# A two-layer graph-attention kernel: transposes of the layers' inputs by VectorE and through DRAM

## The chip, the cores and the metric

The kernel runs on one core of one Trainium2 chip. A core has TensorE (PE, matrix products, with weight loads listed as PEld), VectorE (DVE), ScalarE (ACT), GpSimd (POOL) and SyncE (SP), which here only issues DMAs; each engine works through its own queue in order. The metric is device microseconds of one execution, and lower is better.

## The reference

128 graphs with 128 nodes of 512 features each, all float32, and one adjacency mask per graph. Layer 0 is masked attention with 4 heads of 64, layer 1 is a layer norm with gamma and beta followed by masked attention with 8 heads of 64; in layer 1 each node also sees itself. Each layer adds its input and is normalised.

```python
# layer 0
q, k, v = heads(x @ Wq), heads(x @ Wk), heads(x @ Wv)            # 4 heads of 64
sim  = where(adj, q @ k.T * 64**-0.5, -float32_max)
x    = layernorm(x + (softmax(sim) @ v) @ Wo + bo)
# layer 1
h = (x - mean(x)) * rsqrt(var(x) + 1e-5) * gamma + beta
q, k, v = heads(split(h @ w_qkv.T))                              # 8 heads of 64
sim  = where(adj | eye, q @ k.T * 64**-0.5, -1e9)
out  = layernorm(x + (softmax(sim) @ v) @ w_out.T + b_out)
```

## The kernel before

Work goes in groups of two graphs (`G = 2`, 64 groups). `step(s)` is run for s = 0 to 66 and is a software pipeline written out by hand: the order of the calls in it is the order of the instructions on every engine. In step s layer 0's q, k and v of group s are made (`chunk(0, s, n)`, n = 0 to 3), layer 0's attention runs for group s-1, layer 1's inputs are turned and projected for group s-2 (`transposed(1, s-2)`, `product`), and layer 1's attention runs for group s-3. A step has two halves, one for each graph of the pair; `scores(k)` opens each, with k = 2s and 2s+1.

Within a half, `scores` (L303) makes the score matrices on PE, copies them under the mask on DVE, takes the row maxima, and queues the exponentials for ACT in a list `later`, which `flush` empties: layer 0's exponentials leave inside `scores`, layer 1's at the next `flush()`. `attend(k-1)` (L371) multiplies the previous half's probabilities with v and has ACT copy the result to aT; `normalised(k)` divides by the sums on POOL; `residual(l, k-1)` (L400) multiplies aT with the output weights, adds the input and makes the statistics; `norms` (L435) writes layer 0's result h, or stores layer 1's result y.

PE needs operands with the contracted axis on the partitions, so three things are turned. The probabilities are turned in `blocks` (L351): DVE turns 32 by 32 blocks within their partitions, and sixteen DMAs from SBUF to SBUF put the blocks in their places. The inputs of both layers are turned in `transposed` (L164) by PE against an identity matrix into PSUM, and ACT copies the result to xT, for layer 1 with gamma and beta applied on the way. Layer 1's weights are loaded and turned by PE in `load_transposed` (L101), one block of 128 rows for each call of `p` in the first steps; each block's DMA is issued when its turn comes.

Layer 1's projections are seven products per pair (`product`, L200; a Strassen scheme, in which graph 0 and graph 1 and two halves of the features and weights form 2 by 2 blocks). Each adds into one of three PSUM tiles, named a, c and f in `INTO`. ACT copies tile a out after products 1, 6, 7 and 4, and the later ones add to it. The sums of inputs that they need (`xs`) are made on POOL at the end of `transposed`.

All DMAs are issued by SP, in program order, so one that has to wait holds up all behind it.

Of the kernel before, what the change touches and what calls it, by code (L numbers as in the profile page):

```python
# [10 lines left out]
F32 = mybir.dt.float32  # L11
# [6 lines left out]
P = 128  # L18
# [9 lines left out]
def kernel(ctx: ExitStack, tc: tile.TileContext, x, adj, wq, wk, wv, wo, bo,  # L28
# [11 lines left out]
    two = ctx.enter_context(tc.tile_pool(name="two", bufs=2))  # L40
    three = ctx.enter_context(tc.tile_pool(name="three", bufs=3))
    four = ctx.enter_context(tc.tile_pool(name="four", bufs=4))
    ps_mm = ctx.enter_context(tc.tile_pool(name="ps_mm", bufs=6, space=PSUM))
    ps_st = ctx.enter_context(tc.tile_pool(name="ps_st", bufs=1, space=PSUM))

# [3 lines left out]
    def mm_tile(name):  # L49
        return ps_mm.tile([P, 512], F32, tag="mm", name=name)  # L50
# [4 lines left out]
    def flush(n=0):  # L55
        while len(later) > n:
            later.pop(0)()
# [42 lines left out]

    def load_transposed(dst, src, name, scaled=0):  # L101
        rows, cols = src.shape

        def part(r):
            raw = three.tile([P, cols], F32, tag="h", bufs=10, name=f"{name}_{r}")
            nc.sync.dma_start(raw, src[r * P:(r + 1) * P, :])
            pt = mm_tile(f"{name}t_{r}")
            for c in range(cols // P):
                nc.tensor.transpose(pt[:, c * P:(c + 1) * P], raw[:, c * P:(c + 1) * P], ident)
            to = dst[:, :, r * P:(r + 1) * P]  # L110
            pt = pt.rearrange("p (c f) -> p c f", f=P)
            if r * P < scaled:
                nc.scalar.activation(to, pt, AF.Copy, scale=SCALE)
            elif r % 2:
                nc.scalar.copy(to, pt)
            else:
                nc.vector.tensor_copy(to, pt)

        setup.extend(lambda r=r: part(r) for r in range(rows // P))

    def load_gamma_beta():
        nc.sync.dma_start(gb_raw[:KC], gamma.rearrange("(c p) -> c p", p=P))
        nc.sync.dma_start(gb_raw[KC:], beta.rearrange("(c p) -> c p", p=P))
        pt = mm_tile("gb_t")
        nc.tensor.transpose(pt[:, :2 * KC], gb_raw, ident[:2 * KC, :2 * KC])
        nc.vector.tensor_copy(gb, pt[:, :2 * KC])
# [25 lines left out]
                nc.vector.tensor_sub(t4, b21, t2)  # L152

    load_transposed(w1, w_qkv, "w_qkv", scaled=INNER[1])
    setup.append(load_gamma_beta)
    load_transposed(wo1, w_out, "w_out")
    setup.append(weight_sums)

# [2 lines left out]
    RATIO, H, XT, QK, V = {}, {}, {}, {}, {}  # L161


    def transposed(l, g):  # L164
        if not 0 <= g < NG:
            return
        xT = one.tile([P, KC, T], F32, tag=f"xT{l}", name=f"xT{l}_{g}")
        for c0 in range(0, KC, 2):
            pt = mm_tile(f"xt{l}_{g}_{c0}")
            for c in range(c0, c0 + 2):  # L170
                for b in range(G):
                    src = X[g][:, b] if l == 0 else H[g, b]
                    o = ((c - c0) * G + b) * N
                    nc.tensor.transpose(pt[:, o:o + N], src[:, c * P:(c + 1) * P], ident)  # L174
            if l == 0:
                nc.scalar.copy(xT[:, c0:c0 + 2, :], pt.rearrange("p (c t) -> p c t", t=T))  # L176
            else:
                for c in range(c0, c0 + 2):
                    nc.scalar.activation(xT[:, c, :], pt[:, (c - c0) * T:(c - c0 + 1) * T],  # L179
                                         AF.Identity, bias=gb[:, KC + c:KC + c + 1],  # L180
                                         scale=gb[:, c:c + 1])
        XT[l, g] = xT
        if l == 1:
            xs = one.tile([P, 4, KH, N], F32, tag="xs", name=f"xs_{g}")
            a = xT.rearrange("p (h c) (b n) -> p b h c n", h=2, b=2)
            s1, s2, s3, s4 = (xs[:, i] for i in range(4))
            for o, a0, a1, op in ((s1, a[:, 1, 0], a[:, 1, 1], ALU.add),
                                  (s2, s1, a[:, 0, 0], ALU.subtract),
                                  (s3, a[:, 0, 0], a[:, 1, 0], ALU.subtract),
                                  (s4, a[:, 0, 1], s2, ALU.subtract)):  # L190
                nc.gpsimd.tensor_tensor(o, a0, a1, op=op)
            XS[g] = xs


    XS, ACC, EV = {}, {}, {}
# [69 lines left out]
    def chunk(l, g, n):  # L265

        if not 0 <= g < NG:
            return
        xT = XT[l, g]
        I = INNER[l]  # L270
        nq = I // P
        if n == 0:
            QK[l, g] = two.tile([P, 2 * nq, T], F32, tag=f"qk{l}", name=f"qk{l}_{g}")
            V[l, g] = two.tile([P, G, I], F32, tag=f"v{l}", name=f"v{l}_{g}")
        pm = mm_tile(f"p{l}_{g}_{n}")
        if n < nq:
            for f in (2 * n, 2 * n + 1):
                for c in range(KC):
                    nc.tensor.matmul(pm[:, (f % 2) * T:(f % 2 + 1) * T],  # L279
                                     W[l][:, c, f * P:(f + 1) * P], xT[:, c, :],  # L280
                                     start=(c == 0), stop=(c == KC - 1))
            dst = QK[l, g][:, 2 * n:2 * n + 2, :]
            src = pm.rearrange("p (f t) -> p f t", t=T)
        else:
            b = n - nq
            for c in range(KC):
                nc.tensor.matmul(pm[:, :I], xT[:, c, b * N:(b + 1) * N], W[l][:, c, 2 * I:3 * I],  # L287
                                 start=(c == 0), stop=(c == KC - 1))
            dst, src = V[l, g][:, b, :], pm[:, :I]
        if (n + l) % 2:  # L290
            nc.scalar.copy(dst, src)
        else:
            nc.vector.tensor_copy(dst, src)
# [57 lines left out]
    def blocks(k):  # L351


        both = members(k)
        if not both:
            return
        slots = {0: (0, HEADS[0]), 1: (HEADS[0], HEADS[0] + HEADS[1])}
        t = one.tile([P, 4, sum(HEADS), 32], F32, tag="turned", name=f"turned_{k}")
        pT = one.tile([P, 4, sum(HEADS), 32], F32, tag="pT", name=f"pT_{k}")
        for l, g, b in both:  # L360
            lo, hi = slots[l]
            sm = SM.pop((l, g, b)).rearrange("p s k (q r) -> p q (s k) r", r=32)
            nc.vector.transpose(t[:, :, lo:hi, :], sm)  # L363
            PT[l, g, b] = pT[:, :, lo:hi, :]
        lo, hi = slots[both[0][0]][0], slots[both[-1][0]][1]
        for q in range(4):
            for a in range(4):
                nc.sync.dma_start(pT[32 * q:32 * q + 32, a, lo:hi, :],  # L368
                                  t[32 * a:32 * a + 32, q, lo:hi, :])

    def attend(k):  # L371
        both = members(k)
# [16 lines left out]
    def addend(l, k):  # L389

        for _, g, b in [m for m in members(k) if m[0] == l]:
            if l == 0:
                xin = X[g][:, b, :]
            else:
                xin = H.pop((g, b))
                nc.scalar.activation(xin, xin, AF.Copy, scale=RATIO.pop((g, b)))
            nc.gpsimd.tensor_tensor(xin, xin, (bias0, bias1)[l], op=ALU.add)
            XB[l, g, b] = xin

    def residual(l, k):  # L400
        for _, g, b in [m for m in members(k) if m[0] == l]:
# [4 lines left out]
                nc.tensor.matmul(pm, aT[:, c * P:(c + 1) * P], WO[l][:, c, :],  # L406
                                 start=(c == 0), stop=(c == nk - 1))
            if l == 0:
                y = three.tile([P, E], F32, tag="h", bufs=10, name=f"h_{g}_{b}")
            else:  # L410
                y = two.tile([P, E], F32, tag="y", name=f"y_{g}_{b}")
            nc.vector.tensor_add(y, pm, XB.pop((l, g, b)))  # L412
# [31 lines left out]
    def step(s):  # L444
        def c(n):
            chunk(0, s, n)

        def p(kind, *which, g=s - 2):
            for i in which:
                product(kind, g, i)  # L450
            if setup:
                setup.pop(0)()

        k = 2 * s
        scores(k)
        addend(0, k - 1)
        c(0)
        flush()
        p("", g=-1)
        attend(k - 1)  # L460
        normalised(k)
        addend(1, k - 1)
        c(1)
        p("", g=-1)
        residual(0, k - 1)
        blocks(k)
        p("v", 4, 3, g=s - 3)
        flush()
        residual(1, k - 1)
        transposed(1, s - 2)  # L470
        flush()
        c(2)
        p("qk", 1, 2)
        load(s + 2)
        k += 1
        scores(k)
        addend(0, k - 1)
        p("qk", 6, 5)
        flush()
        attend(k - 1)  # L480
        normalised(k)
        addend(1, k - 1)
        p("qk", 7)
        c(3)
        residual(0, k - 1)
        blocks(k)
        p("qk", 4)
        flush()
        residual(1, k - 1)
        p("qk", 3)  # L490
        flush()
        p("v", 1, 2)
        transposed(0, s + 1)
        p("v", 6, 5, 7)

    transposed(0, 0)
    for s in range(NG + 3):
        step(s)
    assert not setup
# [34 lines left out]
```

## Time and profile before

| | |
|---|---|
| median of 3 runs | 3177.49 us (3176.98 to 3177.89) |
| the profiled execution | 3175.61 us, its span 3173.8 us |
| mean granted TensorE clock | 0.989 |
| busy: PE, DVE, POOL, ACT | 97%, 54%, 43%, 41% of the span |
| matmul instructions | 20801 |
| DMA queue of SP | 159088 packets, 176.84 MB, 19.6% of 16 engines' span |
| transposes of inputs on PE (L174) | 1024, 68.1 us for layer 0 and 67.1 us for layer 1 |

The span runs from the first to the last instruction of that execution. A float32 product takes two matmul instructions (L406 is called 768 times and shows 1536); a transpose takes one. Matmuls are pipelined, so their busy times overlap at the edges; the distance from one start to the next is what one costs in the queue. In the timeline and in the chain of waits, a line gives the start, the length, the engine, the line of the kernel and how many instructions are merged. In the list of DMAs, the last number is the median time from issue to landing.

### The profile page before, as it was taken

To read this page: it belongs to the slowest core of one execution; us is meant where nothing else is said; L and a number is where in the kernel's file an instruction comes from. 1 tells how busy PE (TensorE), PEld (TensorE's weight loads), DVE (VectorE), ACT (ScalarE), POOL (GpSimd) and SP (SyncE) were. 2 spreads that over 40 slices of the span, in tenths; PEclk is the share of its full clock that TensorE was granted. 3 is DMA by queue.
4 is the path that set the end of the run, shared out by engine and by line. 5 is a ranking of instruction groups with operands and counts; after the bars stand their busy time and mean duration, and the time that the engine had idled before them with its cause. 6 is when DMAs were issued, how large, how long until landed. Compare 5 with 4: busy or idle time off the path is not lost.

```text
span 3173.8 us, 57024 instructions
## 1 busy us (share of the span) xinstructions
PE 3092.1 (97%) x20801; PEld 2488.4 (78%) x20801; DVE 1703.0 (54%) x2968; ACT 1285.6 (41%) x4492; POOL 1349.5 (43%) x1799
## 2 busy tenths in 40 slices
PE   5999999999999999999999999999999999999986
PEld 4788878878878878878878878878878888888864
DVE  3355555555555555555555555555555555555553
ACT  2344444444444434434434434444444443443432
POOL 1344444444444444444444444444444444444442
PEclk8999999999999999999999999999999999999998
DMA  3112112112112212212212212212212212212111
GB/s 121 32 54 62 55 53 63 55 52 64 55 51 62 58 50 63 58 49 62 60 48 63 61 48 62 61 48 61 62 48 60 61 50 59 57 54 59 49 42 44
DMA packets 159367, 180.49 MB, mean 57 GB/s; under 512 B 54632, under 2 KB 123760, under 8 KB 159088
## 3 DMA queue, kind: packets, MB, share of 16 engines
q1 hardware_dynamic: 159088, 176.84, 19.6%
q8 instruction: 166, 2.72, 0.4%
q14 instruction: 113, 0.93, 0.1%
HBM read 42.47 MB, written 33.55 MB: 24 GB/s over the span
## 4 chain that ended last, share of the span: by engine, by line
PE 95%; DVE 1%; SPq 1%; ACT 1%; POOL 0%; DMA 0%; issue 0%; POOLq 0%; DVEq 0%; ACTq 0%
PE o L406 21%; PE qka L229 15%; PE p L279 14%; PE qkf L229 7%; PE p L287 7%; PE va L229 7%; PE sc L314 6%; PE av L383 6%; PE qkc L229 3%; PE xt L174 3%; PE vf L229 3%; PE vc L229 2%; SPq L368 1%; ACT sm L339 1%; DVE sm L327 0%
## 5 line engine op out<-in xcount | busy, mean ns | idle before, releaser
L348 POOL TENSOR_TENSOR sm<-sm,rec 128x512 f32<-128x512 f32 (+1 forms) x256 | 376.1, 1469 | 1058.8 <-DVE rec L347 1058.8
L339 ACT ACTIVATE sm<-sm,nmax 128x128 f32<-128x128 f32 x1536 | 595.2, 389 | 488.7 <-DVE nmax L330 434.2
L406 PE MATMUL o<-wo,aT 128*128 128x512 f32 x1536 | 709.7, 598 | 9.2 <-ACT aT L387 9.2
L406 PEld LDWEIGHTS o<-wo,aT 128*128 128x128 f32 x1536 | 289.0, 192 | 270.0 <-issue 248.8
L279 PE MATMUL p<-xT,w 128*128 128x256 f32 x2048 | 478.7, 387 | 1.1 <-ACT xT L176 1.1
L279 PEld LDWEIGHTS p<-xT,w 128*128 128x128 f32 x2048 | 380.5, 191 | 67.0 <-issue 10.8
L419 POOL TENSOR_SCALAR ve<-mv 128x1 f32<-128x1 f32 x256 | 56.0, 219 | 698.5 <-DVE mv L416 698.5
L339 ACT ACTIVATION_READ_ACCUMULATOR sm<-sm,nmax 128x1 f32 x1536 | 286.7, 187 | 0.0
L327 DVE COPY_PREDICATED sm<-m,sc 128x512 f32<-128x512 uint8 (+1 forms) x512 | 270.6, 581 | 25.3 <-PE sc L314 7.4
L229 PEld LDWEIGHTS qkf<-xs,w 128*128 128x128 f32 x2048 | 243.8, 192 | 30.1 <-issue 30.1
L229 PE MATMUL qka<-xs,wsqk 128*128 128x128 f32 x2048 | 262.6, 281 | 0.0
L255 ACT COPY ev<-va 128x256 f32<-128x256 f32 x192 | 71.5, 372 | 460.8 <-PE va L229 443.9
L363 DVE STREAM_TRANSPOSE turned<-sm 128x512 f32<-128x512 f32 (+1 forms) x256 | 235.7, 957 | 35.4 <-issue 27.4
L229 PEld LDWEIGHTS qka<-xs,wsqk 128*128 128x128 f32 x2048 | 238.2, 191 | 18.7 <-issue 10.8
L347 DVE RECIPROCAL rec<-total 128x4 f32<-128x4 f32 (+1 forms) x256 | 47.5, 185 | 378.8 <-ACT sm L339 378.8
L412 DVE TENSOR_TENSOR h<-o,x 128x512 f32<-128x512 f32 x128 | 88.5, 692 | 300.1 <-PE o L406 298.2
L229 PE MATMUL qkf<-xs,w 128*128 128x128 f32 x2048 | 249.4, 275 | 0.0
L330 DVE TENSOR_REDUCE nmax<-sm 128x4 f32<-128x512 f32 (+1 forms) x256 | 244.0, 953 | 8.8
L287 PE MATMUL p<-w,xT 128*128 128x256 f32 x1024 | 246.5, 384 | 0.0
L179 ACT ACTIVATE xT<-xt,gb 128x256 f32<-128x256 f32 x256 | 123.7, 563 | 280.2 <-PE xt L174 280.2
L383 PE MATMUL av<-pT,v 128*64 128x128 f32 x3072 | 198.9, 278 | 24.7 <-DMA pT<-turned 22.4
L383 PEld LDWEIGHTS av<-pT,v 128*64 128x64 f32 x3072 | 167.0, 138 | 55.2 <-issue 40.8
(84 smaller groups left out, 4713.4 us busy)
## 6 DMA issues: line engine op xcount, KB each, us to landing
pT<-turned SPq DMA_DIRECT2D x1984, 48.0 KB, 1.9
x<-in_x_dram SPq DMA_DIRECT2D x64, 512.0 KB, 3.8
out_dram<-y SPq DMA_DIRECT2D x128, 256.0 KB, 2.2
w_qkv<-in_L_gnn_w_qkv_dram SPq DMA_DIRECT2D x12, 256.0 KB, 5.6
m<-in_adj_dram SPq DMA_DIRECT2D x64, 32.0 KB, 3.5
pT<-turned SPq DMA_DIRECT2D x64, 32.0 KB, 1.8
pT<-turned SPq DMA_DIRECT2D x64, 16.0 KB, 1.8
w_out<-in_L_gnn_w_out_dram SPq DMA_DIRECT2D x4, 256.0 KB, 3.2
```

The lines of the kernel that those rows point to most:

```text
L179: nc.scalar.activation(xT[:, c, :], pt[:, (c - c0) * T:(c - c0 + 1) * T], AF.Identity, bias=gb[:, KC + c:KC + c + 1], scale=gb[:, c:c + 1])
L229: nc.tensor.matmul(o, lhsT, rhs, start=first and n == 0, stop=n == len(todo) - 1, skip_group_check=True)
L279: nc.tensor.matmul(pm[:, (f % 2) * T:(f % 2 + 1) * T], W[l][:, c, f * P:(f + 1) * P], xT[:, c, :], start=(c == 0), stop=(c == KC - 1))
L287: nc.tensor.matmul(pm[:, :I], xT[:, c, b * N:(b + 1) * N], W[l][:, c, 2 * I:3 * I], start=(c == 0), stop=(c == KC - 1))
L314: nc.tensor.matmul(ps[h % 2][:, h // 2, :], qk[r, h // 2, t], qk[r, H_ // 2 + h // 2, t], start=True, stop=True)
L327: nc.vector.copy_predicated(sm[:, s], mask[:, None, :].to_broadcast([P, K, N]), ps[s][:, :K, :])
L330: nc.vector.tensor_reduce(nmax, sm, AX.X, ALU.max, negate=True)
L339: nc.scalar.activation(sm[:, s, k, :], sm[:, s, k, :], AF.Exp, bias=nmax[:, s, k:k + 1], accum_out=total[:, s, k:k + 1])
L348: nc.gpsimd.tensor_tensor(sm, sm, rec[:, :, :, None].to_broadcast([P, 2, K, N]), op=ALU.mult)
L363: nc.vector.transpose(t[:, :, lo:hi, :], sm)
L383: nc.tensor.matmul(o.rearrange("p (a r) -> p a r", r=32), v[:, b, h * D:(h + 1) * D], pT[:, :, s * K + kk, :], start=True, stop=True)
L406: nc.tensor.matmul(pm, aT[:, c * P:(c + 1) * P], WO[l][:, c, :], start=(c == 0), stop=(c == nk - 1))
```

## The change

Neither layer's input is turned on PE any more, except group 0 of layer 0 (`first_transposed`). `turn(l, g, b)` has DVE turn 32 by 32 blocks of one graph; after the second graph, `put` stores the whole turned tile (512 KB) to a scratch tile in DRAM with one DMA, and `arrive(l, g)` fetches it into place with four DMAs of 32 partitions each (`fetch`). Layer 0's result is used as it arrives: xT0 has the layout [node, graph, feature block], so that PE reads a column at every eighth float. Layer 1's arrives in a tile `raw`; `finish(g)` applies gamma and beta on ACT, writes xT1 and makes xs on POOL. The probabilities take the same way: one put and four fetches (`probs_arrive`) in place of the sixteen DMAs.

The order in `step` changes with it. All seven v products of a group now run in the first half of the next step, the seven qk products in the second half. Layer 0's `turn` stands after `addend(1, k-1)` of the first half, its `arrive` before `residual(0, k-1)`. Layer 1's graph 0 is turned in the second half of a step, its graph 1 in the first half of the next; `arrive(1, s-2)` follows `probs_arrive` of the first half, and `finish(s-2)` stands between `scores` and `c(2)` of the second. The loads of gamma, beta and all blocks of layer 1's weights are issued before the first step, into buffers that the steps use later.

```diff
 def load_transposed(dst, src, name, scaled=0):
+    raws = []
+    for r in range(rows // P):
+        if name == "w_qkv" and r < 8:
+            raw = three.tile([P, cols], F32, tag="h", bufs=8, name=f"{name}_{r}")
+        else:
+            if r % 4 == 0:
+                four_rows = two.tile([P, 4, cols], F32, tag="qk1", name=f"{name}_{r}")
+            raw = four_rows[:, r % 4]
+        nc.sync.dma_start(raw, src[r * P:(r + 1) * P, :])
+        raws.append(raw)
     def part(r):
-        raw = three.tile([P, cols], F32, tag="h", bufs=10, name=f"{name}_{r}")
-        nc.sync.dma_start(raw, src[r * P:(r + 1) * P, :])
+        raw = raws[r]
...
-def transposed(l, g):            # PE transposes into PSUM, ACT copies to xT (L164-L192)
...
+def put(t, name):
+    scr = dram.tile(list(t.shape), F32, tag=name.split("_")[0], name=name)
+    nc.sync.dma_start(scr, t)
+    return scr
+def fetch(dst, scr):
+    src = scr.rearrange("(a r) q x -> r q a x", r=32)
+    for q in range(4):
+        nc.sync.dma_start(dst[32 * q:32 * q + 32], src[:, q])
+def turn(l, g, b):
+    if b == 0:
+        TURNED[l] = one.tile([P, 4, G * KC * 32], F32, tag=f"turned{l}", name=f"turned{l}_{g}")
+    src = (X[g][:, b] if l == 0 else H[g, b]).rearrange("p (c a i) -> p a c i", a=4, i=32)
+    if l == 0:
+        dst = TURNED[l].rearrange("p a (i b c) -> p a b c i", b=G, c=KC)[:, :, b]
+    else:
+        dst = TURNED[l].rearrange("p a (b c i) -> p a b c i", b=G, c=KC)[:, :, b]
+    nc.vector.transpose(dst, src)
+    if b == G - 1:
+        SCR[l] = put(TURNED[l], f"scr{l}_{g}")
+def arrive(l, g):
+    if l == 0:
+        xT = XT[0, g] = two.tile([P, N, G, KC], F32, tag="xT0", name=f"xT0_{g}")
+        fetch(xT.rearrange("p (a j) b c -> p a (j b c)", a=4), SCR[0])
+    else:
+        RAW[g] = one.tile([P, 4, G, KC, 32], F32, tag="raw", name=f"raw_{g}")
+        fetch(RAW[g].rearrange("p a b c i -> p a (b c i)"), SCR[1])
+def finish(g):
+    raw = RAW[g]
+    xT = XT[1, g] = one.tile([P, KC, T], F32, tag="xT1", name=f"xT1_{g}")
+    for c in range(KC):
+        nc.scalar.activation(xT[:, c, :].rearrange("p (b a j) -> p b a j", b=G, a=4),
+                             raw[:, :, :, c, :].rearrange("p a b j -> p b a j"),
+                             AF.Identity, bias=gb[:, KC + c:KC + c + 1], scale=gb[:, c:c + 1])
...
 def chunk(l, g, n):
-    nc.tensor.matmul(pm[:, (f % 2) * T:(f % 2 + 1) * T],
-                     W[l][:, c, f * P:(f + 1) * P], xT[:, c, :], ...)
+    nc.tensor.matmul(o.rearrange("p (b n) -> p b n", b=G),
+                     W[l][:, c, f * P:(f + 1) * P],
+                     xT[:, :, :, c].rearrange("p n b -> p b n"), ...)
-    nc.tensor.matmul(pm[:, :I], xT[:, c, b * N:(b + 1) * N], W[l][:, c, 2 * I:3 * I], ...)
+    nc.tensor.matmul(pm[:, :I], xT[:, :, b, c], W[l][:, c, 2 * I:3 * I], ...)
...
 def blocks(k):
-    for q in range(4):
-        for a in range(4):
-            nc.sync.dma_start(pT[32 * q:32 * q + 32, a, lo:hi, :], t[32 * a:32 * a + 32, q, lo:hi, :])
+    t, pT = (u[:, :, lo:hi, :].rearrange("p a h i -> p a (h i)") for u in (t, pT))
+    SCR["p"] = pT, put(t, f"scrp{hi - lo}_{k}")
+def probs_arrive(k):
+    if members(k):
+        fetch(*SCR["p"])
...
 def step(s):
     normalised(k)
     addend(1, k - 1)
+    turn(0, s + 1, 0)
+    turn(0, s + 1, 1)
     c(1)
     p("", g=-1)
+    arrive(0, s + 1)
     residual(0, k - 1)
     blocks(k)
-    p("v", 4, 3, g=s - 3)
+    p("v", 1, 2, g=s - 3)
     flush()
+    turn(1, s - 2, 1)
+    probs_arrive(k)
+    arrive(1, s - 2)
+    p("v", 6, 5, g=s - 3)
     residual(1, k - 1)
-    transposed(1, s - 2)
+    p("v", 7, g=s - 3)
     flush()
-    c(2)
-    p("qk", 1, 2)
+    p("v", 4, 3, g=s - 3)
     load(s + 2)
     k += 1
     scores(k)
     addend(0, k - 1)
-    p("qk", 6, 5)
+    finish(s - 2)
+    c(2)
     flush()
     attend(k - 1)
     normalised(k)
     addend(1, k - 1)
-    p("qk", 7)
-    c(3)
+    p("qk", 1)
     residual(0, k - 1)
     blocks(k)
+    p("qk", 2)
+    flush()
+    turn(1, s - 1, 0)
+    probs_arrive(k)
+    p("qk", 6, 5, 7)
+    residual(1, k - 1)
     p("qk", 4)
     flush()
-    residual(1, k - 1)
     p("qk", 3)
-    flush()
-    p("v", 1, 2)
-    transposed(0, s + 1)
-    p("v", 6, 5, 7)
+    c(3)
```

## The prediction

> **What bounds the kernel now.** I read the page first: which engine is busy, and at which clock.
>
> ```profile
> PE 3092.1 (97%) x20801; PEld 2488.4 (78%) x20801; DVE 1703.0 (54%) x2968; ACT 1285.6 (41%) x4492; POOL 1349.5 (43%) x1799
> ...
> PEclk8999999999999999999999999999999999999998
> ```
>
> TensorE (PE) has work 97% of the span at full clock, so a microsecond off its queue counts only while nothing makes it wait. Next I read the chain of work that ended last, in one step in the middle.
>
> ```profile
> 1505.56 1.54 PE sc L314 x24
> 1507.10 3.65 PE p L279 x16
> 1510.74 1.46 PE av L383 x24
> 1512.21 3.65 PE p L279 x16
> 1515.86 1.72 PE o L406 x4
> ...
> 1522.73 0.87 PE xt L174 x8
> ...
> 1528.91 1.54 PE sc L314 x24
> ...
> 1549.91 0.87 PE xt L174 x8
> ```
>
> Every piece is PE. The next step's scores start 47.8 us after 1505.5 (1553.30 in PE's timeline). The xt lines, the transposes of both layers' inputs, are 2 x 0.87 = 1.74 us of it. The third view is the timeline of the second half-step, for what stands behind PE.
>
> ```profile
> 1519.54 1.84 DVE L363 STREAM_TRANSPOSE turned<-sm 128x512 f32<-128x512 f32 x2 [0.22 <-issue]
> ...
> 1521.45 10.93 SPq L368 DMA_DIRECT2D pT<-turned  x16
> ...
> 1523.21 1.93 ACT L179 ACTIVATE xT<-xt,gb 128x256 f32<-128x256 f32 x4 [4.36 <-PE xt L174]
> ...
> 1528.84 1.61 PE L314 MATMUL sc<-qk 64*128 64x128 f32 x24
> ...
> 1531.26 0.40 ACT L339 ACTIVATE sm<-sm,nmax 128x128 f32<-128x128 f32 x1 [3.46 <-DVE nmax L330]
> ...
> 1534.20 0.40 ACT L339 ACTIVATE sm<-sm,nmax 128x128 f32<-128x128 f32 x1 [0.82 <-DVE rec L347]
> ...
> 1537.29 0.83 ACT L387 COPY aT<-av 128x256 f32<-128x256 f32 x2
> ...
> 1539.29 1.02 PE L406 MATMUL o<-wo,aT 128*128 128x512 f32 x2
> ```
>
> The reader should see ScalarE's (ACT's) order: layer 0's exponentials begin 2.42 us after the scores, layer 1's at 5.36, aT is copied at 8.45, and PE needs it only at 10.45. That slack of 1.6 us (the layer-0 copy takes 0.35) exists because qk products 6, 5 and 7 and a chunk stand between the scores and o. The sixteen pT DMAs take 10.93 us to issue and just make the next attend.
>
> **The change part by part.** I count t from a step's first scores, u from its second.
>
> *Transposes off PE.* 127 of 128 groups go: -1.74 us a step. ACT loses layer 0's copies (L176, 68.8 us in all); they lay beside PE and gain nothing. VectorE (DVE) gains four transposes a step of 0.71 us (the 128x512 row of L363). Layer 0's two fall into 3.36 us in which DVE waits for o (t=8.8 to 12.2), so cost nothing; layer 1's follow the h norm.
>
> *Product order, first half.* All seven v products now follow o of layer 0 (0.865 each). Product 4 stands directly behind 7 and adds to the same PSUM tile that ACT must copy first. Product 7's matmuls end 1.03 us after they start, ACT starts 0.09 later (1505.56 to 1505.65 in that timeline) and takes 0.37, so with a hand-over product 4 starts at 1.55 instead of 0.865: +0.7. The first half is 1.54+3.65+1.46+3.65+1.72+7x0.865+3.43 = 21.5, so u=0 is t=22.2.
>
> *Product order, second half.* Between scores and o stand only c(2), attend and product 1: 1.54+1.73+1.46+1.78 = 6.5 us. ACT's order is layer 0's exponentials, the four of `finish`, layer 1's exponentials, aT. This is the wait that replaces the transposes. At the earliest: 3.98 (layer 0 done) + 1.93 (L179 x4) + 3.09 (layer 1, 1534.20 to 1537.29) + 0.35 + 0.1 hand-over = 9.45. Floor of the stall: 2.9 us a step.
>
> *The trip through DRAM.* `finish` also needs layer 1's raw tile, behind everything on SP's queue. Its prices have these rows:
>
> ```profile
> x<-in_x_dram SPq DMA_DIRECT2D x64, 512.0 KB, 3.8
> out_dram<-y SPq DMA_DIRECT2D x128, 256.0 KB, 2.2
> ...
> w_out<-in_L_gnn_w_out_dram SPq DMA_DIRECT2D x4, 256.0 KB, 3.2
> ```
>
> A put of 512 KB is the 256 KB store's 2.2 plus 256 KB at 347 GB/s (319 GB/s at a share of 0.92 in the first 20 us) = 2.95; of 768 KB, 3.7. An issue is 0.63 (sixteen in 10.1 to 10.9). Layer 0's turned tile is ready at t=10.25, put by 13.2, its four fetches issued by 15.75. The probabilities' put starts when blocks ends (t=15.9) and lands at 19.6; layer 1's put is queued at 17.6 (after the h norm and 0.71). Eight fetches follow, probabilities first: the last starts at 19.6+7x0.63 = 24.0. A 256 KB load lands in 3.2, a 48 KB pT copy in 1.9; I take 3.2, the one that reads DRAM. Probabilities land at 24.7, before attend at u=3.27 (t=25.5): hidden, by 0.8. Layer 1 lands at 27.2, u=5.0. Then o is at 5.0+1.93+3.09+0.35+0.1 = 10.5 and the stall **4.0 us** a step.
> The ends: 2.9 where raw lands before u=3.98. At the other, DVE's strided writes doubled (+1.4), puts of 3.8 and 4.5 (the 512 KB load's price), landings of 3.8 and issues of 0.68: layer 1 lands near t=31.3, u=9.1, stall 8.1. The odd half's probabilities have some 5 us to spare and are hidden.
>
> *The clock.* The 4.0 us are two gaps: before product 1 (1.3, for `finish`'s first two pieces) and before o (about 2.6). PE's timeline shows what gaps do:
>
> ```profile
> 134.53 0.98 PE L174 MATMUL xt<-ident,h 128*128 128x128 f32 x7 [2.78 <-DVE h L437]
> 135.35 3.27 PE L287 MATMUL p<-w,xT 128*128 128x256 f32 x8
> ...
> 3129.53 3.70 PE L406 MATMUL o<-wo,aT 128*128 128x512 f32 x8 [2.32 <-ACT aT L387]
> ```
>
> After 2.78 us idle the granted clock fell to 0.50 for some 3 us and eight matmuls took 3.27 instead of 1.89; after 2.32 us it did not fall. A gap between the two pays about 1.5 us in half of the steps: +0.75; ends 0 and 1.65. [...]
>
> *Strided columns.* Layer 0's xT0 has a column every 8 floats; no operand of before is read so. Ends: nothing, or the 32 matmuls of c(0) and c(1) doubled, +7.3 us a step, plus about 1.3 in c(3) for strided weight loads; 64 steps give +550. I take nothing, since the nearest row, pT read in runs of 32 (av: 198.9 us for 3072 matmuls; the contiguous sc: 207.5 for 3072), shows no surcharge for a split pattern; that row is far. [...]
>
> *Weights in one go.* In the first 75 us PE waited 11.2 us for gamma/beta and 15.7 us for w_out, both queued on SP behind pT issues. They now come before any put. A first put, fetch and attend trip with no work over it takes some back: -20 us; ends 0 and -35.
>
> *Sum.* 61 steps hold both layers and c(2): 61 x (-1.74 + 0.7 + 4.0 + 0.75) = +226. With -20: 3175.6 (the profiled execution) + 206 = 3381.6. The median of the runs shown is 1.9 above that execution, so 3384.
>
> **The rivals.**
> *Faster: the wait before o does not appear.* Then 127 x 0.87 = 110 and 20 at the start come off, and 64 x 0.7 = 45 for product 4 stay: 3177.5-110-20+45, about 3092. It decides where ACT delivers aT within 7.5 us of the second scores, 1.04 after PE asks: the point at which wait plus 0.7 equals 1.74. Against it: even before, with no `finish` in ACT's queue, aT of layer 0 was not copied before 8.45+0.35 = 8.8. For it: nothing in these rows, only the chance that a piece of PE's queue is longer than summed.
> *Little slower: only the floor.* Raw is there by u=3.98 and the clock stays up: 61 x (-1.74+0.7+2.9) = +113, start -35: about 3255. Both puts would have to land in little more than the 256 KB store's 2.2.
> *Strided columns cost.* 3384 + 550 = 3935 for a full doubling, about 3620 for half. For: eight floats between columns is the new thing in PE's reading. Against: pT's split runs.
> *DRAM trips much later.* Stall 8.1 and the clock loss in every step: 61 x 8.7 = +531, about 3709.
>
> **How the numbers follow.** Forecast as summed 0.62, its own range 3255 to 3710; strided columns 0.22 (3600 to 3935); between no change and 3255, 0.08; faster 0.07; within 0.2% (about what a measurement of this kernel can tell from no change) 0.01. So slower has 0.92. From 3240 to 3830 leaves out faster, most of the little-slower case and the top of the strided one: just under 2 in 10.
>
> **What would show it.** Right: the waits list ACT aT under PE's o near the scores' second half, some 2 to 3 us in about 61 places, and PE's product 1 on ACT's xT; ACT's `finish` waits for the DMA of raw; a v product waits 0.7 for ACT; PE's share falls to about 90% with DVE near 1880 us busy; the step is some 51.5 us. Strided cost: c(0) takes over 3.7 us for its 16. Wrong: if aT is early, or raw lands before u=4. If attend waits for pT, the put is dearer than 3.7.

## The result and the profile after

The changed kernel takes 3889.23 us (median of 4 runs, 3877.59 to 3894.92) against 3177.55 before: 1.2235 times as long, 95% interval 1.2206 to 1.2264, or 712 us more. The forecast, 3384 in 3240 to 3830, had the direction and missed the size; the time lies above the range, 46 us under the 3935 of the rival that strided columns cost. The profiled execution took 3891.53 us, its span 3889.7.

First the page's busy times and its row of the granted clock.

```profile
PE 3610.7 (93%) x19785; PEld 2500.5 (64%) x19785; DVE 1923.8 (49%) x3223; ACT 1239.9 (32%) x4365; POOL 1349.3 (35%) x1799
...
PEclk9999999999999999999999999999999999999998
```

PE runs 1016 matmul instructions fewer (the transposes) and is busy 519 us longer, at a clock that is nine tenths or more in all of these coarse slices but the last. So most of the loss is no wait: single instructions have become longer. The groups, with shapes kept apart, say which (sum, mean ns of one, idle time before them and what ended it); first three of them before, then after:

```profile
L279 PE MATMUL p<-xT,w 128*128 128x256 f32 x2048 | 478.7, 387 | 1.1 <-ACT xT L176 1.1
...
L287 PE MATMUL p<-w,xT 128*128 128x256 f32 x1024 | 246.5, 384 | 0.0
...
L287 PEld LDWEIGHTS p<-w,xT 128*128 128x128 f32 x1024 | 187.6, 193 | 20.9
```

```profile
L330 PE MATMUL p<-xT,w 128*128 128x256 f32 x2048 | 976.0, 645 | 3.0 <-ACT xT L221 3.0
L460 PE MATMUL o<-wo,aT 128*128 128x512 f32 x1536 | 745.9, 623 | 169.3 <-ACT aT L441 169.3
...
L339 PE MATMUL p<-w,xT 128*128 128x256 f32 x1024 | 286.7, 423 | 0.0
...
L339 PEld LDWEIGHTS p<-w,xT 128*128 128x128 f32 x1024 | 255.5, 335 | 8.9 <-issue 1.0
```

L330 (L279 before) makes layer 0's q and k and streams xT0 as its moving operand: 478.7 us and 387 ns before, 976.0 and 645 now. L339 (L287) has xT0 as the loaded weights: a load takes 335 ns instead of 193, and its 1024 matmuls are 40 us busier. Together that is 538 us of the 712. Most of the rest is in the waits (engine, tile and line, releaser, us in all, times, longest); before, o waited 9.2 us for aT in all:

```profile
PE o L460 <- ACT aT L441: 169.3, 67, 5.8
...
ACT xT L231 <- DMA raw<-scr: 59.0, 57, 13.3
...
PE va L279 <- ACT ev L305: 37.5, 65, 4.4
...
PE qka L279 <- ACT xT L231: 33.5, 39, 2.8
...
PE av L437 <- DMA pT<-scrp: 19.7, 8, 6.0
```

These are the waits that the prediction named, in its places: about one a step before o for aT, of 2.5 us on average, `finish` for raw, a v product for ACT, and in 39 steps product 1 for `finish`; the probabilities' trip is on time but for 8 places. PE's timeline shows both kinds of loss in one step.

```profile
2022.56 1.61 PE L366 MATMUL sc<-qk 64*128 64x128 f32 x24
2024.10 7.62 PE L330 MATMUL p<-xT,w 128*128 128x256 f32 x16
2031.65 1.53 PE L437 MATMUL av<-pT,v 128*64 128x128 f32 x24
2033.11 7.62 PE L330 MATMUL p<-xT,w 128*128 128x256 f32 x16
2040.56 1.90 PE L460 MATMUL o<-wo,aT 128*128 128x512 f32 x4
...
2049.18 1.03 PE L279 MATMUL va<-wsv,xs 128*128 128x256 f32 x4
2050.72 1.13 PE L279 MATMUL va<-wsv,xT 128*128 128x256 f32 x4 [0.52 <-ACT ev L305]
...
2052.64 1.61 PE L366 MATMUL sc<-qk 64*128 64x128 f32 x24
2054.18 2.29 PE L339 MATMUL p<-w,xT 128*128 128x256 f32 x8
2056.40 1.53 PE L437 MATMUL av<-pT,v 128*64 128x128 f32 x24
2057.90 2.32 PE L279 MATMUL qka<-xT,w 128*128 128x128 f32 x16
2062.70 3.45 PE L460 MATMUL o<-wo,aT 128*128 128x512 f32 x4 [2.48 <-ACT aT L441]
2065.99 1.95 PE L279 MATMUL qkc<-xT,w 128*128 128x128 f32 x16
...
2082.26 1.61 PE L366 MATMUL sc<-qk 64*128 64x128 f32 x24
```

The step is 59.7 us long (2022.56 to 2082.26) where it was 47.8. Start to start, c(0) takes 7.55 and c(1) 7.45 instead of 3.65 and 3.55: +7.8. c(2) takes 2.22, c(3) 2.12 (from 2080.14) instead of 1.73: +0.9. Product 4 begins 1.54 after product 7 instead of 0.865: +0.7. Product 1 and the wait for aT take 4.80 instead of 1.78: +3.0. o of layer 0 takes 3.29 instead of 1.72, at a lower clock: +1.6. Less 1.74 for the transposes this makes +12.3, against a step that is 11.9 longer. From the seventh load of x on SP to the last, their mean distance, which is the mean step, is 59.4 us, 47.81 before.

### The profile page after: what moved, and what is told of

Same layout as the page of the kernel before. It is cut to its first block, busy times and chain, and to the rows that moved or that the text cites. A ratio compares the mean times of both kernels' runs of the same rounds, so it can differ in the third digit from the quotient of the medians.

```text
span 3889.7 us, 54015 instructions
## 1 busy us (share of the span) xinstructions
PE 3610.7 (93%) x19785; PEld 2500.5 (64%) x19785; DVE 1923.8 (49%) x3223; ACT 1239.9 (32%) x4365; POOL 1349.3 (35%) x1799
## 4 chain that ended last, share of the span: by engine, by line
PE 73%; ACT 8%; DMA 8%; DVE 4%; SPq 4%; issue 2%; POOL 1%; ACTq 0%; DVEq 0%; POOLq 0%
PE p L330 24%; PE o L460 18%; PE qka L279 9%; DMA raw<-scr 6%; PE qkf L279 6%; ACT sm L391 5%; SPq L186 4%; PE qkc L279 3%; PE p L339 3%; ACT xT L231 3%; PE va L279 3%; PE sc L366 2%; PE av L437 2%; PE vf L279 1%; PE vc L279 1%
## 5 line engine op out<-in xcount | busy, mean ns | idle before, releaser
L330 PE MATMUL p<-xT,w 128*128 128x256 f32 x2048 | 976.0, 645 | 3.0 <-ACT xT L221 3.0
L460 PE MATMUL o<-wo,aT 128*128 128x512 f32 x1536 | 745.9, 623 | 169.3 <-ACT aT L441 169.3
L330 PEld LDWEIGHTS p<-xT,w 128*128 128x128 f32 x2048 | 414.3, 207 | 469.7 <-issue 458.5
L339 PE MATMUL p<-w,xT 128*128 128x256 f32 x1024 | 286.7, 423 | 0.0
L305 ACT COPY eqk<-qka 128x512 f32<-128x512 f32 x192 | 111.4, 580 | 498.6 <-PE qka L279 498.6
L339 PEld LDWEIGHTS p<-w,xT 128*128 128x128 f32 x1024 | 255.5, 335 | 8.9 <-issue 1.0
L491 DVE TENSOR_SCALAR y<-y,mv,rstd 128x512 f32<-128x512 f32 x128 | 201.8, 1576 | 106.4 <-POOL rstd L480 106.4
L279 PE MATMUL qka<-xs,wsqk 128*128 128x128 f32 x2048 | 249.8, 275 | 2.1 <-ACT eqk L305 2.1
L279 PE MATMUL qkf<-xs,w 128*128 128x128 f32 x2048 | 249.7, 275 | 0.0
L279 PEld LDWEIGHTS qka<-xs,wsqk 128*128 128x128 f32 x2048 | 239.0, 192 | 2.3 <-issue 2.3
L279 PEld LDWEIGHTS qkf<-xs,w 128*128 128x128 f32 x2048 | 239.0, 192 | 0.0
L466 DVE TENSOR_TENSOR y<-o,h 128x512 f32<-128x512 f32 x128 | 88.6, 692 | 270.5 <-PE o L460 261.8
```

The source lines that it names most:

```text
L279: nc.tensor.matmul(o, lhsT, rhs, start=first and n == 0, stop=n == len(todo) - 1, skip_group_check=True)
L305: nc.scalar.copy(e, src)
L330: nc.tensor.matmul(o.rearrange("p (b n) -> p b n", b=G), W[l][:, c, f * P:(f + 1) * P], xT[:, :, :, c].rearrange("p n b -> p b n"), start= ...
L339: nc.tensor.matmul(pm[:, :I], xT[:, :, b, c], W[l][:, c, 2 * I:3 * I], start=(c == 0), stop=(c == KC - 1))
L491: nc.vector.tensor_scalar(y, y, mv[:, 0:1], r[:, n:n + 1], op0=ALU.subtract, op1=ALU.mult)
```

## The experiments

Three theories were open once this was seen. **Reading:** a column of xT0 lies every eight floats, and PE pays for each element of such an operand, whatever else goes on. **Traffic:** c(0) and c(1) are slow because transfers and DVE's strided writes use the same memory at the time. **Order:** apart from that, the loss comes from ACT's queue and the trip of raw, as predicted, and a different order takes it back. Times are medians, each against the kernel before on the same chip (3176.37 for the first four, 3177.65 for reordered2 and probs_dram, 3176.15 for the others).

**The stride alone, in the kernel before.** PE still transposes and no transfer is added; only ACT's copy of layer 0's transposed input writes another layout, and c(0) to c(3) read it.

```diff
-        xT = one.tile([P, KC, T], ...)                       # a column is 128 adjacent floats
+        xT = one.tile([P, N, G, KC], ...)                    # strided8: one float in 8
-  xT[:, c, :]                     xT[:, c, b * N:(b + 1) * N]
+  xT[:, :, :, c] (as p b n)       xT[:, :, b, c]
   # strided4: [P, G, N, KC], one float in 4;  strided2: [P, G, KC//2, N, 2], one float in 2
```

> The kernel before, with PE transposes and all, but ACT writes layer 0's xT as [node, graph, feature block], so that c(0) to c(3) read a column at every 8th float. Theory A (the column step doubles a float32 matmul): 16 matmuls of c(0) and of c(1) take 7.55 us instead of 3.65, c(2) and c(3) 2.1 instead of 1.73, so 64 x (2 x 3.9 + 2 x 0.4) = +550: about 3725 us. Theory B (the matmuls are slow after the change because the operand is written by DMAs, or because of the DMA traffic of 414 MB): no change here, 3165 to 3190 us.

> The same with a column at every 4th float (16 bytes). Theory A, if what counts is that each column touches another 16-byte line: as with 8 floats, about 3725 us. If the cost grows with the step: between, about 3300 to 3600. Theory B: 3165 to 3190.

> The same with a column at every 2nd float (8 bytes). Theory A with 16-byte lines, two columns in each: about 3178 us, unchanged. If any step costs: about 3725. Theory B: 3165 to 3190.

strided8 took 3728.94 us, 1.1739 [1.1722, 1.1757] of before: +552.6. strided4 took 3707.93, 1.1677 [1.1658, 1.1697]. strided2 took 3195.96, 1.0064 [1.0049, 1.0079]. The groups by shape, of strided8:

```profile
L280 PE MATMUL p<-xT,w 128*128 128x256 f32 x2048 | 975.8, 645 | 2.8 <-ACT xT L176 2.8
L288 PEld LDWEIGHTS p<-w,xT 128*128 128x128 f32 x1024 | 256.3, 334 | 1.0
L176 ACT COPY xT<-xt 128x512 f32<-128x512 f32 x128 | 130.3, 1128 | 53.5 <-PE xt L174 53.5
```

of strided4:

```profile
L280 PE MATMUL p<-xT,w 128*128 128x256 f32 x2048 | 959.4, 636 | 2.7 <-ACT xT L176 2.7
```

and of strided2:

```profile
L280 PE MATMUL p<-xT,w 128*128 128x256 f32 x2048 | 498.4, 395 | 2.7 <-ACT xT L176 2.7
L288 PEld LDWEIGHTS p<-w,xT 128*128 128x128 f32 x1024 | 193.3, 199 | 16.4
```

With none of the change's traffic strided8 has the changed kernel's 645 ns to the nanosecond, so traffic falls and reading stands. The price is no slope but a step: two columns in 16 bytes add 4% of busy time (498.4 us against 478.7 for adjacent floats), one in 16 bytes doubles it (959.4), and one in 32 bytes costs little more (975.8). A mean matmul takes 395, 636 and 645 ns in these three rows, with 387 for adjacent floats. The expectations' theory of 16-byte lines fits them; that it is lines which count was not shown, since only distances of 8, 16 and 32 bytes were run. ACT's doubled copy (1128 ns instead of 589) cost almost nothing in time: PE's wait for ACT's copy of a v tile is 10.6 us in all in strided8.

**The changed kernel with straight columns.** Layer 0's turned blocks are stored as layer 1's are, fetched in runs of 32 floats, and DVE copies them into adjacent columns (434 ns a graph), behind its own turn of layer 1.

```diff
-            dst = TURNED[l].rearrange("p a (i b c) -> p a b c i", b=G, c=KC)[:, :, b]
+            dst = TURNED[l].rearrange("p a (b c i) -> p a b c i", b=G, c=KC)[:, :, b]
...
+    def straighten(g):
+        xT = XT[0, g] = two.tile([P, G, KC, N], F32, tag="xT0", ...)
+        for b in range(G):
+            nc.vector.tensor_copy(xT[:, b].rearrange("p c (a i) -> p a c i", a=4), RAW0[g][:, :, b])
...
         turn(1, s - 2, 1)
+        straighten(s + 1)
```

> The changed kernel, but layer 0's turned input is fetched in runs of 32 nodes into the tile that raw uses, and DVE copies it (two copies of 128x512 a step, some 1.4 us, in the first half) to an xT0 with adjacent columns. Theory A: c(0) and c(1) back at 3.65 us each and c(2), c(3) at 1.73; the wait of o for aT grows by the 0.4 that c(2) no longer takes; 3889 - 64 x (7.8 + 0.4) = about 3365 us, which is near the forecast without strided columns, 3384. Theory B: c(0) stays near 7.5 us where DMA traffic is the cause, about 3890; back at 3365 where it was the DMA-written operand, as DVE now writes it.

It took 3395.91 us, 1.0691 [1.0675, 1.0707] of before: 493 less than the changed kernel (the two were run apart), and 12 from the forecast of 3384, which took the columns for free. The same group of matmuls, and then its waits:

```profile
L333 PE MATMUL p<-xT,w 128*128 128x256 f32 x2048 | 482.3, 389 | 2.3 <-ACT xT L224 2.3
```

```profile
PE o L463 <- ACT aT L444: 170.2, 67, 5.8
PE qka L282 <- ACT xT L234: 56.5, 64, 3.3
PE va L282 <- ACT ev L308: 37.5, 65, 4.4
```

The matmuls are back at 389 ns and the waits stay. The columns are worth 8.7 us a step by the pieces above; the step shrinks by 8.1 (59.4 to 51.31), in part since the wait before product 1 grows (33.5 to 56.5 us) as the half in front of it no longer gives raw so much time. What is left, +3.5 us a step over before, is the part that the prediction had summed.

**Product 7 away from product 4.** In the straightened kernel, which this edit and those of finish_late and reordered start from, layer 1's v product 7 goes ahead of o of layer 1, so that product 4 need not wait for ACT's copy.

```diff
         p("v", 6, 5, g=s - 3)
-        residual(1, k - 1)
         p("v", 7, g=s - 3)
+        residual(1, k - 1)
         flush()
```

> The kernel 'straightened' with v product 7 moved ahead of o of layer 1, so that 3.43 us of work stand between products 7 and 4 and the pause of 0.68 us before product 4 goes. If each pause of PE costs by itself: 3396 - 64 x 0.68 = about 3352 us. If layer 1's raw tile, whose landing is tied to the first half's o, is what `finish` and so aT and o of the second half wait for: the second scores come 0.68 us sooner and the wait after them grows by as much, about 3396 us, no change.

3396.85 us, 1.0694 [1.0679, 1.0708]: nothing. The waits of PE say where it went.

```profile
PE o L463 <- ACT aT L444: 151.0, 67, 6.0
PE qka L282 <- ACT xT L234: 97.1, 63, 2.8
...
PE va L282 <- ACT ev L308: 5.0, 2, 4.4
```

The v products' wait is gone (37.5 to 5.0) and product 1's has grown (56.5 to 97.1). Layer 1's second turn follows layer 0's o and the norm of the first half, so raw comes at a fixed distance from that o; PE, now earlier at the scores, waits longer for the same transfer. In the middle of the run the second scores come 0.8 us sooner after the first ones (21.5 instead of 22.3), and product 1 starts 28.1 us after the first ones in both kernels (medians of PE's timeline). The pause of 0.7 lay beside a transfer and was worth nothing by itself. Smaller shifts cancel: o's wait is 19 us shorter, attend's waits are 15 longer, and the mean clock is 0.971 instead of 0.978.

**`finish` later.** ACT gets `finish` behind the copies of aT, and PE gets c(3) in front of attend in place of product 1.

```diff
-        finish(s - 2)
         c(2)
+        c(3)
         flush()
         attend(k - 1)
         normalised(k)
+        finish(s - 2)
         addend(1, k - 1)
-        p("qk", 1)
         residual(0, k - 1)
         blocks(k)
+        p("qk", 1)
...
-        c(3)
```

> The kernel 'straightened' with `finish` behind the copies of aT in ACT's queue, c(3) moved up to stand behind c(2), and qk product 1 behind o and blocks. Theory: o waits for aT because of ACT's queue (exponentials, `finish`, raw's landing). Then aT is copied 8.45 to 8.8 us after the second scores, PE asks after 1.54+1.73+1.73+1.46 = 6.46, one wait of 2.4 us is left in place of about 4.3 (1.0 before product 1, 2.5 before o, the rest in product 1): 3396 - 61 x 1.9 = 3280 us, and about 3240 if the clock falls less often. Rival: the DRAM trip itself bounds the step (raw or the probabilities land too late wherever `finish` stands): within 20 us of 3396.

3380.84 us, 1.0644 [1.0629, 1.0658]: a miss; over 100 us were expected and 15 came. Its waits, from the list of waits of PE:

```profile
PE o L463 <- ACT aT L444: 179.0, 69, 6.1
...
PE sc L369 <- DVE qk L313: 16.1, 63, 0.3
PE qka L282 <- ACT xT L234: 6.0, 1, 6.0
```

Product 1's wait is gone (56.5 to 6.0), but o's is as long as it was: o starts 9.23 us after the second scores instead of 10.83, and PE asks for it as much sooner, since product 1 and its wait no longer stand in front. With `finish` out of the way layer 1's exponentials and the copies of aT still need about 9 us. On average over the middle steps o comes 1.5 us sooner after the second scores, near the 1.9 that were expected, but two other pieces lose most of that again. Layer 0's scores now wait halfway for DVE's addition, so c(0) starts 2.06 us after the first scores instead of 1.54. And from o to the next scores PE takes 19.2 us on average instead of 18.4, because the clock is lower more often. Of the pauses of over 1 us before o, 25 of 64 are followed by an o of layer 0 at a lower clock in the straightened kernel (its four matmuls take over 2.4 us in PE's timeline, on average 1.59 more than the usual 1.9), and 51 of 65 here (1.53 more), with the pause the same 2.5 us; the mean clock is 0.966, in the straightened kernel 0.978.

The records of the granted clock show most of why pauses of one length differ. In each of seven executions (before, changed, straightened, v_apart, finish_late and the two reordered ones) all stretches of lower clock begin on one grid of 3.41 us, and all but the last of each last 3.41 us or a multiple of it. In finish_late 58 of the 59 stretches follow a grid interval in which PE was busy for 0.375 or less of the time, and of all other intervals at full clock none, after the first 5 us, is under 0.41. So in finish_late a pause of 2.5 us was followed by a lower clock where it left PE busy for 0.375 or less of one interval (idle for some 2.1 us of it, as 3.41 x 0.625), and not where the grid cut it more evenly. Two cases from finish_late, the pause from 2023.31 to 2025.82 and the one from 2073.19 to 2075.70 (grid interval, its length, PE's busy time and instructions, granted clock, DMA share and GB/s):

```profile
2021.90:2025.31 3.41, 1.41 (x24) 1.00 0.24 77
2025.31:2028.72 3.41, 2.90 (x14) 1.00 0.00 0
2073.10:2076.51 3.41, 0.90 (x4) 1.00 0.05 9
2076.51:2079.92 3.41, 3.41 (x10) 0.50 0.00 0
```

The straightened kernel shows the same: 33 of its 35 stretches follow intervals of 0.414 or less, and of the others at full clock none, after the first 10 us, is under 0.412. But in v_apart 15 of 37 stretches follow intervals of 0.51 to 0.53, so the busy share of one interval is not the whole rule. Which pauses fall within an interval depends on how the steps line up with the grid; no run shifts them alone.

**Other work between scores and o.** For the wait to go, PE needs more to do there than ACT needs time. With `finish` late as in the last edit and product 7 ahead as in v_apart, two v products and o of layer 1 move from the first half to behind the second scores, and c(3) goes between attend and o. The diff is against finish_late.

```diff
         p("v", 6, 5, g=s - 3)
-        residual(1, k - 1)
         p("v", 7, g=s - 3)
-        flush()
-        p("v", 4, 3, g=s - 3)
         load(s + 2)
         k += 1
         scores(k)
+        p("v", 4, 3, g=s - 3)
+        residual(1, k - 2)
         addend(0, k - 1)
         c(2)
-        c(3)
         flush()
         attend(k - 1)
         normalised(k)
         finish(s - 2)
         addend(1, k - 1)
+        c(3)
         residual(0, k - 1)
```

> As 'finish_late', and v products 4 and 3 and the first half's o of layer 1 moved behind the second scores, c(3) between attend and o: 10.1 us of PE work then stand between the second scores and o, which needs aT at 8.9. If the waits behind the second scores are all that is left of the loss: a step of 46.05 us against 47.8 before, 3177 - 63 x 1.74 = about 3070 us, faster than before. If the probabilities' trip is then the bound (they land near t=24.9, attend asks at t=24.8): 0 to 1.5 us a step more, 3070 to 3165. If the DRAM traffic bounds: above 3177.

3118.81 us, 0.9819 [0.9805, 0.9832] of before: 57 us faster than the kernel before and the fastest of all orders tried. That is in the range of the expectation's second case, but pT is only a small part of why. In PE's timeline the second half has no pause for ACT left:

```profile
2009.34 1.61 PE L369 MATMUL sc<-qk 64*128 64x128 f32 x24
2010.87 1.13 PE L282 MATMUL va<-wsv,xT 128*128 128x256 f32 x4
...
2018.57 1.53 PE L440 MATMUL av<-pT,v 128*64 128x128 f32 x24 [0.23 <-DMA pT<-scrp]
2020.03 1.99 PE L342 MATMUL p<-w,xT 128*128 128x256 f32 x8
2021.86 1.88 PE L463 MATMUL o<-wo,aT 128*128 128x512 f32 x4
```

```profile
PE av L440 <- DMA pT<-scrp: 41.1, 24, 9.0
PE sc L369 <- DVE qk L313: 16.1, 63, 0.3
PE o L463 <- ACT aT L444: 14.2, 5, 5.7
```

o starts 12.5 us after the scores and finds aT ready; its 170 us of waits are 14, and the mean clock is 0.990. The mean step is 47.08 us, 0.7 under before. The transposes were worth 1.74; of the other 1.0, half goes to the first scores, which wait halfway for DVE's addition (c(0) 2.06 us after them instead of 1.54), some 0.2 to pT, and the rest to small pauses between products, above all of the two v products behind the second scores (2.15 us instead of 1.73). The 57 us are not the transposes' alone: 0.73 in each of 61 steps is 45, and the rest lies at the start and the end, where the two parts tried alone below gain as well.

**A second order.** To give DVE and the transfers still more time, c(1) goes behind v product 7 (from step 4 on; earlier steps keep it in place), and products 1, 2 and 6 go ahead of o of layer 0. The diff is against reordered.

```diff
-        c(1)
-        p("", g=-1)
+        if s < 4:
+            c(1)
+        p("v", 1, 2, g=s - 3)
+        p("v", 6, g=s - 3)
         arrive(0, s + 1)
         residual(0, k - 1)
         blocks(k)
-        p("v", 1, 2, g=s - 3)
+        p("v", 5, g=s - 3)
...
-        p("v", 6, 5, g=s - 3)
         p("v", 7, g=s - 3)
+        if s >= 4:
+            c(1)
```

> As 'reordered', but from step 4 on c(1) stands behind v product 7 and v products 1, 2 and 6 take its place before o of the first half: o comes 1.05 us sooner, and the probabilities' trip with it, and 3.65 us stand between product 7 and the scores. If the small waits left in 'reordered' are for pT (0.2 a step) and for ACT behind product 7 (0.3): 3119 - 61 x 0.5 = about 3090 us. If o then waits for aT (asked at 9.25, ready at 8.9 to 9.0) or the weights of the pipeline's other waits take their place: 3110 to 3130.

3206.07 us, 1.0085 [1.0071, 1.0099]: a miss, 87 us behind reordered (run apart). The waits of PE have one that was not expected:

```profile
PE va L282 <- ACT ev L308: 103.9, 63, 5.2
```

Product 6 adds to the tile that ACT must copy after product 1, and that copy now stands in ACT's queue behind exponentials: 1.5 us in one step (at 2007.20), and 1.5 on average over the middle steps. That is more than the whole loss: 61 x 1.5 = 92 us.

**The loads in one go.** In the kernel before, the DMAs of gamma, beta and layer 1's weights are issued ahead of the first step instead of one by one within the steps.

```diff
+        for r in range(rows // P):          # before the first step
+            raw = ...
+            nc.sync.dma_start(raw, src[r * P:(r + 1) * P, :])
+            raws.append(raw)
         def part(r):
-            raw = three.tile([P, cols], F32, tag="h", bufs=10, ...)
-            nc.sync.dma_start(raw, src[r * P:(r + 1) * P, :])
+            raw = raws[r]
...
```

> The kernel before with one part of the change alone: the loads of gamma, beta and layer 1's weights issued before the first step. If the two waits of PE (11.2 us for gamma/beta, 15.7 us for w_out) go and nothing takes their place: about 3150 us; the prediction's term of -20 for the start (from which a put and fetch trip was taken off) stands with 3150 to 3160. If other waits of the first steps take their place: 3165 to 3178.

3163.45 us, 0.9960 [0.9946, 0.9974]: 12.7 less. The waits of 11.2 and 15.7 us for these loads are gone from PE's list, which begins

```profile
PE av L394 <- DMA pT<-turned: 38.5, 8, 8.6
```

where it had 22.4 before: with 26.9 us of waits gone from the start, attend waits 16.1 us longer for its probabilities, 15.4 of it in two places in the first 70 us. The mean step is unchanged (47.82 us).

**The probabilities' trip alone.** In the kernel before, one store to DRAM and four fetches take the place of the sixteen DMAs.

```diff
+        nc.sync.dma_start(scr, t)
+        src = scr.rearrange("(a r) q x -> r q a x", r=32)
         for q in range(4):
-            for a in range(4):
-                nc.sync.dma_start(pT[32 * q:32 * q + 32, a, lo:hi, :], t[32 * a:32 * a + 32, q, lo:hi, :])
+            nc.sync.dma_start(pT[32 * q:32 * q + 32], src[:, q])
```

> The kernel before with one part of the change alone: the probabilities go by one put to DRAM and four fetches instead of sixteen DMAs between SBUF tiles. If the trip is hidden behind PE in every full step, as the prediction has it (put 3.3 and fetch 3.5 as the changed kernel's profile shows them, some 8.6 us against the 12.8 that sixteen issues and a landing took): within 15 us of 3176, the small gain from the first and last steps, where PE waits for pT. If the trip is later than the sixteen DMAs where it matters: 0.5 us a step or more, 3205 us and up.

3158.73 us, 0.9942 [0.993, 0.9955]: 18.9 less, a little more than expected. In PE's waits the trip is hidden (22.4 us before), and the loads behind the shorter row of issues come sooner (the wait for w_out was 15.7 us before; that for gamma and beta, 11.2 us before, is 5.5); o's waits for aT take some back (20.8 us in 7 places, 9.2 before). The mean step hardly changes, 47.75 us against 47.81, so most of the gain lies at the start and the end:

```profile
...
PE w_outt L110 <- DMA w_out<-in_L_gnn_w_out_dram: 9.7, 1, 9.7
PE av L386 <- DMA pT<-scrp: 7.6, 2, 4.4
```

## Why the prediction was wrong in size, point by point

**Strided columns: the step that failed.** The prediction took nothing for them, "since the nearest row, pT read in runs of 32 [...] shows no surcharge for a split pattern". That row was no neighbour: its single floats are adjacent and only its runs are apart, while in xT0 each float is 32 bytes from the next. Alone, the columns cost 552.6 us (strided8), which is the upper end that the prediction had written (+550) to half a per cent. Of the measured excess of 712, removing them takes back 493 and leaves 219.5 (3395.91 less 3176.37), where the sum was +206. The error was one of choice: 0.62 and 0.22 were given the wrong way round, and the range stopped short of the case that came.

**Transposes off PE, -1.74 a step: right.** They are gone from the queue (1016 matmul instructions fewer), and where other work hides the new waits, in reordered, the step is 0.7 us shorter than before. No run takes the transposes off without waits that the change brings with it. DVE's turns of layer 0 take 1.08 us each, not the 0.71 they were put at.

**Product 4 behind 7, +0.7: right in place and size, but no cost that can be saved alone.** The timeline shows 0.68. In the sum it is not counted twice: the second scores were put at t=22.2 with the 0.7 in it, and raw's landing at t=27.2 does not move with it, so without the 0.7 the next term would have been 4.7. v_apart shows just that: the pause goes and the wait for raw grows by as much.

**o waits for aT, +4.0: right.** The forecast had o at 10.5 us after the second scores; it starts at 10.06 in the changed kernel and 10.83 in the straightened one in one step of each, at 10.5 and 10.7 on average over the middle steps. Raw was put at 5.0 and was there at 5.4 (straightened, where ACT's `finish` starts at 2043.29 after scores at 2037.92). The gaps were put at 1.3 and 2.6 and measure 1.03 and 2.49 in the straightened kernel.

**The clock, +0.75: right in size, not in its reason.** 25 of the 64 pauses of the straightened kernel are followed by an o that is on average 1.6 us longer: 40 us, or 0.6 a step; in the changed kernel 27 of 64. The prediction compared the lengths of two gaps, 2.78 and 2.32 us, and took one between them to pay in half of the steps. The length does not decide it: the same 2.5 us pay in 25 cases and not in 39, by where they lie on the grid of 3.41 us (see the runs with `finish` later). That the share came near a half is luck; in finish_late it is 51 of 65.

**The trips through DRAM: right in result, off in prices.** The probabilities are in time in all but 8 places; alone their trip gains 18.9. Puts take 3.0 (512 KB) and 3.3 us (768 KB), put at 2.95 and 3.7. Fetches land in 3.1 to 4.7, put at 3.2; an issue of a fetch takes 0.44, put at 0.63. The errors nearly cancel (seven issues 1.3 us shorter, raw's landing 1.5 longer), and that raw's arrival came out right is in part luck.

**Weights in one go, -20: too much.** The first scores of step 3 start at 117.6 us in the changed kernel and 117.9 before, and 113.5 in the straightened one: -4 without the columns. weights_early alone gains 12.7.

**The rivals.** *Faster* failed as the changed kernel stands: aT comes 2.5 us too late, not within 1.04. With more in PE's queue between scores and o, which is what reordered made, the wait before o does go, and the kernel is faster than before. *Little slower* and *trips much later* did not come: raw was where it was put. *Strided columns cost* came.

## What to carry to other kernels

Before the transposed layout of an operand is chosen, look at the distance of single elements along which TensorE reads: one float in each 16 bytes doubled the busy time of the products here (959.4 us instead of 478.7), and a DVE copy of 0.43 us a graph bought that back. A wait before a product is closed by what stands in front of it on the engine that waits, not only by hastening what it waits for: taking ACT's `finish` out gained 0.4%, putting PE's other products there as well gained 8% over the straightened order. A pause that lay beside a transfer saved nothing when it was taken away (v_apart: 3396.85 us, and 3395.91 with the pause), since a later wait ended with that transfer. And what a pause costs in clock is not read from its length alone: 2.5 us were followed by a lower clock in 25 of 64 cases in one order and in 51 of 65 in another.

## What the runs showed of the hardware that was not expected

- The price of a step between floats jumps: a mean matmul takes 387 ns on adjacent ones, 395 at 8 bytes, 636 at 16, 645 at 32 (128x256 moving operand); as loaded weights 193, 199, 327 and 334 ns.
- Writers pay too: ACT's copy of 128x512 took 589 ns into adjacent floats, 633, 1123 and 1128 at 8, 16 and 32 bytes; DVE's transpose of x, 128x512, took 1077 ns with writes 32 bytes apart in the changed kernel and 665 with adjacent ones in the straightened one.
- A pause of 2.5 us on PE was followed by a lower clock in 25 of 64 cases in one order of the work and in 51 of 65 in another. The lower clock starts and ends on a grid of 3.41 us, and in the second order it comes after intervals of the grid with PE busy for 0.375 or less and, but for one, never after more. In v_apart it also comes after intervals of 0.51 to 0.53; what counts there is open.
